# Two-dimensional long convolution with channel whitening: two buffers each for x and y, smaller y pieces, two-sided single groups and filler matmuls

## The chip, the cores and the metric

The kernel runs on one core of a Trainium2 chip. A core has a matrix engine (TensorE, PE in the profile), three engines for elementwise work (VectorE or DVE, ScalarE or ACT, GpSimd or POOL), a queue engine SP that issues transfers, and 16 DMA engines that move bytes between the device memory and the on-chip memory of 128 partitions. The metric is the time of one execution on the device, in microseconds. Lower is better.

## The reference

Everything is float32. The input `x` has 4 images, 64 channels and 256 x 256 pixels. Two small networks make a filter for each channel: `hx` and `hy`, 256 taps each. The kernel of a channel is their outer product, so the two-dimensional causal convolution separates into one along the rows and one along the columns. A second layer decorrelates the channels.

```
def filter(z, w1, b1, w2, b2, w3, b3, wo, freq):
    h = sin(freq * (z @ w1 + b1))
    h = sin(freq * (h @ w2 + b2))
    h = sin(freq * (h @ w3 + b3))
    return (h @ wo) * decay

k = outer(hx, hy) per channel                      # 256 x 256
y = irfft2(rfft2(x, 512) * rfft2(k, 512) / 512)[:256, :256] + x * bias

x1 = y with channels first, (64, 4*256*256)
x1_s = x1[:, ::9]                                  # every ninth pixel
mean1 = mean(x1_s)
cov = x1_s @ x1_s.T / n + 0.01 * I                  # x1_s as it is, mean not taken off
deconv = inverse square root of cov, five Newton-Schulz steps
out = deconv @ (x1 - mean1), back as (4, 64, 256, 256)
```

## The kernel before

**Filters.** At the start, six matmuls (line 147) with sines between them make the taps of all channels; two more (line 162) finish them. The taps go to device memory, as the array `g_d` and, for the first two channels, `g0_d` (lines 164 to 166).

**Convolution.** A convolution with 256 taps is a product with a triangular Toeplitz matrix. `load_toeplitz` (line 173) reads overlapping rows of the taps so that each partition holds a shifted copy. Channels come in 8 blocks of 8 (`g`), a block's matrices being one tile of a pool of three buffers. A step is one block of one image, `(g, n)`; there are 32. In the step order, blocks 0 to 5 run over the four images each; then each image has blocks 6 and 7. A step has four positions, `c` = 0, 2, 4, 6, of two channels each. In this text, (28, 4) is position c = 4 of step number 28.

At each position `group` (line 320) runs two jobs at once on TensorE. The first is the product along one axis for the present item (`p1`), the second is the product along the other axis for the item two positions earlier (`p2`). `toeplitz_products` (line 188) puts one job on the upper 64 rows of the array and the other on the lower 64 and swaps them with each tap block `k`. The order of `k` alternates from group to group. Between tap blocks a GpSimd no-op (line 224) keeps two halves from writing to the same bank at once. ScalarE copies `p1` to the tile `o1` with its halves swapped (line 338); VectorE adds `x * bias` to `p2` and writes `y` (line 343). VectorE also takes the samples for the covariance with nine masked copies for each step (line 252), some after each group. The first two groups have no second job and the last two no first job. In those, one half of the array has nothing to do at any time.

**Queues.** Within the convolution every engine keeps the order of the program text. After the instructions of a group, SP issues the store of `y` for the second item (line 353), then one load of `x` (line 103), then, in some groups, a Toeplitz load (line 178) and an early load of a finished piece of `y` (line 290). A DMA instruction waits on SP until its source is ready and its target free, and all that stands behind it waits too. `x` and `y` have three buffers each. The `x` load issued at c = 2 of step i is the first quarter of step i + 2:

```
part = (c - 2) // 2 % 4
to = i + 2 if c else i + 1
```

**Whitening.** After the last step come the last covariance (line 266) and a chain of small products, which give the matrix `W`. `y` is then read back in 32 pieces of 128 partitions by 4096 columns (2 MB), two images in one array `y_d[v]`, 64 channels each. `homes` (line 280) lists 13 buffers, by then unused by the convolution, for the first 13 pieces. Eight are loaded while the convolution still runs, at the positions in `early` (line 311), five after it. For each piece TensorE multiplies by `W` (line 521), ScalarE and VectorE add the shift (lines 526 and 529), and GpSimd issues the store to the output (line 534). A buffer is loaded again when its store is done.

Of the kernel before, what the change touches and what calls it, by code (L numbers as in the profile page):

```python
# [37 lines left out]
F32 = mybir.dt.float32  # L38
I32 = mybir.dt.int32
AF = mybir.ActivationFunctionType  # L40
ALU = mybir.AluOpType
AX = mybir.AxisListType
AFTER = mybir.DependencyInfo(mybir.DependencyClass.Sync, mybir.DependencyReason.DATA)

NB, C, L = 4, 64, 256
P, H2 = 128, 2
EMB, ORDER = 33, 64
PIX = L * L
CG = 8
HP = P // 2  # L50
# [5 lines left out]
GW = P + L  # L56
FP = 4096
# [8 lines left out]
def conv_whiten_kernel(ctx: ExitStack, tc: tile.TileContext, a: dict, out: bass.AP):  # L66
    nc = tc.nc
    x = a["x"]

    const = ctx.enter_context(tc.tile_pool(name="const", bufs=1))  # L70
    big = ctx.enter_context(tc.tile_pool(name="big", bufs=3))
    spool = ctx.enter_context(tc.tile_pool(name="spool", bufs=NB))
    tpool = ctx.enter_context(tc.tile_pool(name="tpool", bufs=3))
    o1pool = ctx.enter_context(tc.tile_pool(name="o1pool", bufs=4))
    dram = ctx.enter_context(tc.tile_pool(name="dram", bufs=1, space=bass.MemoryType.DRAM))
    psA = ctx.enter_context(tc.tile_pool(name="psA", bufs=8, space=bass.MemoryType.PSUM))

    y_d = [dram.tile([2 * C, PIX], F32, tag=f"y{v}", name=f"y_d{v}") for v in range(NB // 2)]
    g_d = dram.tile([P, GW], F32, tag="g", name="g_d")
    g0_d = dram.tile([2, 2, GW], F32, tag="g0", name="g0_d")  # L80

# [56 lines left out]
    nc.scalar.activation(bf[:, 1:2], bf[:, 0:1], AF.Sin)  # L140
    freq = cols[:, 3:4]
    nc.vector.tensor_scalar(bf, cols[:, 0:3], freq, None, ALU.mult)
    hs, wt = [zw[:, u * P : (u + 1) * P] for u in range(2)], zw[:, L : L + P]
    for i in range(3):
        for u in range(2):
            pm = psA.tile([P, P], F32, tag="psA", name=f"pm{i}_{u}")
            nc.tensor.matmul(pm, lhsT=wt, rhs=hs[u], start=True, stop=True)  # L147
            half = slice(u * P, (u + 1) * P)
            arg, k, nxt = (scratch[:, 2 + 3 * i + v, half] for v in range(3))
            nc.scalar.activation(arg, pm, AF.Identity, bias=bf[:, i : i + 1], scale=freq)  # L150
            nc.vector.tensor_scalar(k, arg, 1.0 / (2.0 * math.pi), MAGIC, ALU.mult, ALU.add)
            nc.vector.tensor_scalar(k, k, MAGIC, None, ALU.subtract)
            for part in (TP1, TP2):
                nc.vector.scalar_tensor_tensor(arg, k, -part, arg, ALU.mult, ALU.add)  # L154
            nc.vector.tensor_scalar(arg, arg, 3.1415925, -3.1415925, ALU.min, ALU.max)
            nc.scalar.activation(nxt, arg, AF.Sin)  # L156
            hs[u] = nxt
        wt = wbd[:, i * P : (i + 1) * P]
    for u in range(2):
        half = slice(u * P, (u + 1) * P)  # L160
        pf = psA.tile([P, P], F32, tag="psA", name=f"pf{u}")
        nc.tensor.matmul(pf, lhsT=wt, rhs=hs[u], start=True, stop=True)
        nc.vector.tensor_tensor(taps[:, half], pf, decay[:, half], ALU.mult)
    for f, queue in enumerate((nc.sync, nc.scalar)):
        queue.dma_start(out=g0_d[f], in_=taps[f * C : f * C + 2])
    nc.scalar.dma_start(out=g_d, in_=taps)

    def new_toeplitz(g):

# [1 line left out]
        return tpool.tile([P, 2, CG, L], F32, tag="toep", name=f"toep_{g}")  # L171

    def load_toeplitz(t, g, f, half, lo=0, hi=CG):
        source, row = (g0_d, 2 * f) if g == 0 and hi == 2 else (g_d, f * C + g * CG + lo)


        skip = 0 if f == half else HP
        nc.sync.dma_start(
            out=t[half * HP : (half + 1) * HP, f, lo:hi, skip:],
            in_=bass.AP(  # L180
                tensor=source.tensor,
                offset=source.offset + row * GW + skip,
                ap=[[1, HP], [GW, hi - lo], [1, L - skip]],
            ),
        )


    def toeplitz_products(units, ks):
# [3 lines left out]
        for k in ks:  # L192

            w = HP if k == L // HP - 1 else P
            for u, unit in enumerate(units):
                ends = []
                for m in range(H2):
                    for q in range(0, P, w):
                        for low in range(2):


                            job = unit[(k + low) % 2]
                            if job is None:
                                continue
                            ps, src, t = job
                            parts = slice(low * HP, (low + 1) * HP)
                            stop = HP * k - 1 if k else None
                            mm = nc.tensor.matmul(  # L208
# [13 lines left out]
                if k != ks[-1]:  # L222

                    fence[u] = nc.gpsimd.nop()  # L224
                    for name in ends:
                        tc.add_manual_dep(fence[u].ins, name, AFTER, reason="row tiles")

    def pack_by_pe(g, n, yt, cs):

# [30 lines left out]
    def covariance(n):  # L260
# [13 lines left out]
        nc.vector.scalar_tensor_tensor(cov, pc, 1.0 / NSAMP, cov, ALU.mult, ALU.add)  # L274


    pieces = [(v, q) for v in range(NB // 2) for q in range(PIX // FP)]


    homes = [  # L280
        {"t": (tpool, "toep"), "s": (spool, "samp"), "i": (big, "in"), "o": (big, "out")}[k]
        for k in "tssioitsoitos"
    ]

    def load_y(i):

        v, q = pieces[i]
        pool, tag = homes[i % len(homes)]
        t = pool.tile([P, FP], F32, tag=tag, name=f"yi_{v}_{q}")
        nc.sync.dma_start(out=t, in_=y_d[v][:, q * FP : (q + 1) * FP])  # L290
        return t

    def load_next():
# [6 lines left out]
    def bank(name):  # L300
        return psA.tile([P, H2, L], F32, tag="psA", name=name)
# [6 lines left out]
            k = first + (part * 12 // 8 if g < C // CG - 2 else part)  # L308
            blocks[k // 4, k % 4 * 2] = (g, part)

    early = {(28, 4): 1, (28, 6): 1, (29, 6): 1, (30, 4): 1, (31, 2): 1, (31, 4): 1, (31, 6): 2}
    orders = [list(range(L // HP)), list(reversed(range(L // HP)))]

    def pack(time=math.inf):
        while todo and time > 0:
            cost, op = todo.pop(0)
            op()
            time -= cost

    def group(first, second):  # L320

        units = [[None, None] for _ in range(2)]
        for u in range(2):
            if second is not None:
                g, n, c, _, _, o1s = second
                units[u][1] = (bank(f"p2_{g}_{n}_{c + u}"), o1s[u], toep[g][:, 1, c + u, :])
            if first is not None:
                g, n, c, xt, _, _ = first
                units[u][0] = (bank(f"p1_{g}_{n}_{c + u}"), xt[:, c + u], toep[g][:, 0, c + u, :])

        toeplitz_products(units, orders[0])
        orders.reverse()
        for u in range(2):
            if first is not None:
                g, n, c, _, _, o1s = first
                o1 = o1pool.tile([P, H2, L], F32, tag="o1", name=f"o1_{g}_{n}_{c + u}")
                for to, fr in ((slice(0, HP), slice(HP, P)), (slice(HP, P), slice(0, HP))):
                    nc.scalar.copy(o1[to], units[u][0][0][fr])  # L338
                o1s.append(o1)
            if second is not None:  # L340
                g, n, c, xt, yt, _ = second
                ch = g * CG + c + u
                nc.vector.scalar_tensor_tensor(  # L343
                    yt[:, c + u], xt[:, c + u], bias[:, ch : ch + 1], units[u][1][0],
                    ALU.mult, ALU.add,
                )

        pack(2.5)
        if second is not None:
            g, n, c, _, yt, _ = second  # L350
            last = (g, n) == steps[-1]
            row = n % 2 * C + g * CG + c
            nc.sync.dma_start(
                out=y_d[n // 2][row : row + 2, :].rearrange(
                    "c (b p w) -> p (c b) w", p=P, w=L
                ),
                in_=yt[:, c : c + 2].rearrange("p c b w -> p (c b) w"),
            )
            if last and c == CG // 2 - 2 or not last and c == CG - 2:
                todo.extend(pack_ops(g, n, yt, slice(0, c + 2)))  # L360

    engines = mybir.EngineType
    with tc.manual_schedule(
        engines={engines.PE, engines.SP, engines.DVE, engines.Activation, engines.Pool}
    ):
        toep = {0: new_toeplitz(0)}
        for lo, hi in ((0, 2), (2, CG)):
            for part in range(4):
                load_toeplitz(toep[0], 0, part // 2, part % 2, lo, hi)
        for c in range(0, CG, 2):  # L370
            load_x(loaded_x[steps[1]], *steps[1], c)
        for i, (g, n) in enumerate(steps):
            xt = loaded_x.pop((g, n))
            yt = big.tile([P, CG, H2, L], F32, tag="out", name=f"y_{g}_{n}")
            for c in range(0, CG, 2):
                item = (g, n, c, xt, yt, [])
                if g == C // CG - 1 and n > 0 and c == 4:
                    covariance(n - 1)
                group(item, pending.pop(0) if len(pending) == 2 else None)
                pending.append(item)  # L380
                if i == 0 and c == 6:

# [3 lines left out]
                    for u in range(2):  # L386
                        nc.vector.tensor_copy(twice[:, u], ident[0:C, 0:C])

                part = (c - 2) // 2 % 4
                to = i + 2 if c else i + 1  # L390
                if to < len(steps) and to > 1:
                    if part == 0:
                        loaded_x[steps[to]] = new_x(*steps[to])
                    load_x(loaded_x[steps[to]], *steps[to], 2 * part)
# [7 lines left out]
                    load_next()  # L402
        g, n, c, xt, yt, _ = pending[0]
        for item in pending:
            group(None, item)

        pack()
        pack_by_pe(g, n, yt, slice(CG // 2, CG))
# [95 lines left out]


    halves = [slice(u * C, (u + 1) * C) for u in range(2)]
    for i, (v, q) in enumerate(pieces):
        yt = loaded.pop(i)
        o = out[2 * v : 2 * v + 2].rearrange("u c h w -> (u c) (h w)")[:, q * FP : (q + 1) * FP]

        part = FP if 1 < i < len(pieces) - 2 else FP // 4
        for w in range(FP // 1024):


            po = [
                psA.tile([P, 512], F32, tag="psA", name=f"po_{v}_{q}_{w}_{u}") for u in range(2)
            ]
            cols = [slice((2 * w + k) * 512, (2 * w + k + 1) * 512) for k in range(2)]
            for k in range(2):
# [73 lines left out]
```

## Time and profile before

| | |
|---|---|
| median of 3 runs | 928.11 us (927.27 to 928.23) |
| the profiled execution | 930.36 us, span 928.2 us |
| PE busy | 788.6 us, 85% |
| DVE busy | 653.6 us, 70% |
| ACT busy | 480.9 us, 52% |
| DMA | 285.56 MB, mean 308 GB/s |
| first convolution matmul | 20.72 us |
| last convolution group's bias-add | 636.63 us |
| first whitening product | about 664 us |

The span is the part of an execution that the profile covers. Digits in a slice row are tenths of 1/40 of the span (23.2 us). An engine name with a q, such as SPq, stands for its queue of DMA instructions. A busy PE is not always PE at its best, since the time of one matmul in the trace includes its latency; matmuls that follow each other closely overlap. The clock row holds what the records of granted clock say; the first such record lies at about 40 us, and what came before is to be read from the spacing of the matmuls.

### The profile page before, as it was taken

The numbers are of one execution on the slowest core, as the hardware profiler recorded it, in microseconds if no ns is written. First come the engines' busy times: TensorE is split into PE (matmuls) and PEld (weight loads), VectorE is DVE, ScalarE is ACT, GpSimd is POOL, SyncE is SP. The second block draws the span as 40 slices with busy tenths as digits, with TensorE's granted clock in tenths as the row PEclk, the third lists the DMA queues.
The fourth block names the chain that finished last, engine by engine and source line by source line (L and its number), as shares of the span: only waits on it lengthen the run. The fifth ranks groups of instructions, "written<-read, shape, count | busy, mean of one in ns | idle before, by whom it ended". The sixth has DMA issues, their size and how long they took to land.

```text
span 928.2 us, 27807 instructions
## 1 busy us (share of the span) xinstructions
PE 788.6 (85%) x11814; PEld 631.0 (68%) x11814; DVE 653.6 (70%) x869; ACT 480.9 (52%) x791; POOL 31.8 (3%) x71
## 2 busy tenths in 40 slices
PE   3999999999999999999999999999787777765400
PEld 2899999999999999999999999998311111111100
DVE  3058687768777877787677866667599999996500
ACT  2345454545454544554554544441399888876500
POOL 3000000000000000000000000000010000000010
PEclk9999999999999999999999999999799999998755
DMA  4698888888888888879997769989999999999998
GB/s 145 189 275 257 251 258 261 248 258 258 252 251 262 260 248 261 262 237 280 284 277 236 234 189 332 326 288 392 417 407 429 430 428 429 431 430 431 431 430 340
DMA packets 115406, 285.56 MB, mean 308 GB/s; under 512 B 6831, under 2 KB 89172, under 8 KB 107604
## 3 DMA queue, kind: packets, MB, share of 16 engines
q1 hardware_dynamic: 108080, 216.08, 70.2%
q0 software_dynamic: 6336, 67.11, 17.0%
q8 instruction: 93, 1.52, 0.7%
q10 hardware_dynamic: 868, 0.60, 0.2%
q14 instruction: 29, 0.24, 0.1%
HBM read 149.35 MB, written 134.42 MB: 306 GB/s over the span
## 4 chain that ended last, share of the span: by engine, by line
PE 69%; issue 15%; DVE 9%; ACT 3%; DMA 2%; POOL 0%; POOLq 0%; ACTq 0%; DVEq 0%; SPq 0%
PE p L208 65%; DVE yi L529 8%; ACT yi L526 3%; DMA yi<-y_d 2%; PE pc L266 2%; PE pk L234 1%; POOL out_dram L534 0%; PE po L521 0%; DMA toep<-g_d 0%; DVE y L343 0%; PE ZY L436 0%; PE YT L436 0%; DVE scratch L154 0%; DVE samp L252 0%; PE pm L147 0%
## 5 line engine op out<-in xcount | busy, mean ns | idle before, releaser
L208 PE MATMUL p<-toep,x 64*64 64x64 f32 (+3 forms) x5120 | 595.6, 288 | 5.2 <-DMA toep<-g_d 4.7
L208 PE MATMUL p<-toep,o 64*64 64x64 f32 (+3 forms) x5120 | 589.2, 285 | 0.2
L208 PEld LDWEIGHTS p<-toep,x 64*128 64x128 f32 (+1 forms) x5120 | 548.3, 168 | 31.5 <-issue 5.6
L208 PEld LDWEIGHTS p<-toep,o 64*128 64x128 f32 (+1 forms) x5120 | 543.5, 166 | 11.8 <-POOLq L224 0.6
L338 ACT COPY o<-p 64x512 f32<-64x512 f32 x512 | 297.0, 580 | 317.9 <-PE p L208 310.1
L343 DVE SCALAR_TENSOR_TENSOR y<-x,bias,p 128x512 f32<-128x512 f32 x256 | 179.9, 743 | 162.7 <-PE p L208 162.2
L252 DVE COPY_PREDICATED samp<-mask,y 128x448 f32<-128x448 int32 (+3 forms) x288 | 281.0, 976 | 6.6
L529 DVE TENSOR_SCALAR yi<-po,shift 64x512 f32<-64x512 f32 x256 | 192.1, 750 | 23.4 <-PE po L521 16.7
L521 PE MATMUL po<-yi,W 64*64 64x512 f32 x1024 | 150.0, 653 | 63.1 <-DVE yi L529 40.9
L526 ACT ACTIVATE yi<-po,shift 64x512 f32<-64x512 f32 x256 | 174.9, 683 | 42.4 <-PE po L521 34.9
L521 PEld LDWEIGHTS po<-yi,W 64*64 64x64 f32 x1024 | 35.4, 141 | 176.9 <-DVE yi L529 127.8
L534 POOL DMA_DIRECT2D out_dram<-yi x44 | 23.7, 539 | 262.6 <-DVE yi L529 119.3
L420 POOL MEMSET chain<- 64x64 f32 x1 | 0.1, 146 | 616.6 <-PE p L208 616.6
L266 PEld LDWEIGHTS pc<-samp 128*64 128x64 f32 x464 | 14.4, 137 | 2.2 <-issue 1.4
L266 PE MATMUL pc<-samp 128*64 128x65 f32 x464 | 15.1, 223 | 0.7 <-ACT samp L243 0.4
L147 PE MATMUL pm<-scratch 128*128 128x128 f32 (+1 forms) x12 | 3.7, 466 | 8.8 <-ACT scratch L156 6.2
L274 DVE SCALAR_TENSOR_TENSOR cov<-pc,cov 128x65 f32<-128x65 f32 x4 | 0.9, 226 | 12.7 <-PE pc L266 12.7
L147 PEld LDWEIGHTS pm<-scratch 128*128 128x128 f32 (+1 forms) x12 | 2.9, 313 | 9.4 <-ACT scratch L156 6.8
L234 PE MATMUL pk<-y,pick 128*128 128x112 f32 (+1 forms) x36 | 7.7, 390 | 1.3 <-DVE y L343 1.3
L234 PEld LDWEIGHTS pk<-y,pick 128*128 128x128 f32 x36 | 7.3, 259 | 1.7 <-issue 1.7
L243 ACT COPY samp<-pk 128x116 f32<-128x116 f32 x1 | 0.3, 271 | 15.9 <-PE pk L234 15.9
L131 POOL TENSOR_SCALAR pick<-ident,rows 128x128 f32<-128x128 f32 x9 | 5.7, 649 | 0.0
(71 smaller groups left out, 41.8 us busy)
## 6 DMA issues: line engine op xcount, KB each, us to landing
x<-in_x_dram SPq DMA_DIRECT2D x128, 512.0 KB, 5.8
y_d<-y SPq DMA_DIRECT2D x128, 512.0 KB, 4.1
yi<-y_d SPq DMA_DIRECT2D x32, 2048.0 KB, 16.0
out_dram<-yi POOLq DMA_DIRECT2D x28, 2048.0 KB, 43.4
out_dram<-yi POOLq DMA_DIRECT2D x16, 512.0 KB, 8.4
toep<-g_d SPq DMA_DIRECT2D x28, 256.0 KB, 6.3
toep<-g_d SPq DMA_DIRECT2D x28, 192.0 KB, 5.7
toep<-g_d SPq DMA_DIRECT2D x2, 384.0 KB, 8.3
```

Source lines behind the costliest of these rows:

```text
L131: nc.gpsimd.tensor_scalar(pick[:, s, :], ident, rows[:, s : s + 1], None, ALU.mult)
L147: nc.tensor.matmul(pm, lhsT=wt, rhs=hs[u], start=True, stop=True)
L208: mm = nc.tensor.matmul(ps[q : q + w, m, HP * k : L], lhsT=src[parts, k // 2, m * P + q : m * P + q + w], rhs=t[parts, : stop : -1] if k e ...
L234: nc.tensor.matmul(pk[:, b, :, 0:nj], lhsT=pick[:, (s - b) % STEP, :], rhs=yt[:, cs, b, s : s + STEP * (nj - 1) + 1 : STEP], start=(s == 0 ...
L252: nc.vector.copy_predicated(dst, m, src)
L266: nc.tensor.matmul(pc[half], lhsT=samp[n][:, b, j, 0:C], rhs=samp[n][:, b, j, :], start=(b == 0 and j < 2), stop=(b == H2 - 1 and j >= NJ ...
L338: nc.scalar.copy(o1[to], units[u][0][0][fr])
L343: nc.vector.scalar_tensor_tensor(yt[:, c + u], xt[:, c + u], bias[:, ch : ch + 1], units[u][1][0], ALU.mult, ALU.add,)
L521: nc.tensor.matmul(po[u][halves[k]], lhsT=W[halves[u]], rhs=yt[halves[u], cols[k]], start=True, stop=True,)
L526: nc.scalar.activation(yt[halves[0], cols[k]], po[0][halves[k]], AF.Identity, bias=shift[halves[k]])
L529: nc.vector.tensor_scalar(yt[halves[1], cols[k]], po[1][halves[k]], shift[halves[k]], None, ALU.add)
L534: nc.gpsimd.dma_start(out=o[:, end - part : end], in_=yt[:, end - part : end])
```

## The change

- `x` and `y` (the tags "in" and "out") have two buffers each for three. The memory that this frees is a new pool of two tiles, which the convolution never uses; they are the first two of the 13 homes.
- `y_d` is one array for each image, with the upper and lower half of the image as the two sets of 64 partitions. A piece belongs to one image. Early loads start at (26, 4), two steps sooner; there are still eight. The store of `y` in a group becomes two DMAs, one for each half. The output has the same layout as these arrays and is put in order on the host.
- The `x` load after a group is now for the next step at c = 4 and 6, and for the present step at c = 0 and 2.
- The two first and two last groups use `half_group`, which puts both channels of the only job on both halves of the array at once, in four banks, with a fence for each bank.
- Block 0's Toeplitz matrices come in 14 loads of two or four channels in the order in which the groups use them, for 8. `g0_d` is stored by one DMA.
- Between the filter layers TensorE multiplies a tile of zeros: 8, 10 and 9 times, and 20 times after the last.

```
-    big = ctx.enter_context(tc.tile_pool(name="big", bufs=3))
+    big = ctx.enter_context(tc.tile_pool(name="big", bufs=2))
+    epool = ctx.enter_context(tc.tile_pool(name="epool", bufs=2))
-    y_d = [dram.tile([2 * C, PIX], F32, tag=f"y{v}", name=f"y_d{v}") for v in range(NB // 2)]
+    y_d = [dram.tile([H2 * C, PIX // H2], F32, tag=f"y{n}", name=f"y_d{n}") for n in range(NB)]
...
+    idle = o1pool.tile([P, H2 * L], F32, tag="o1", name="idle")
+    nc.vector.memset(idle, 0.0)
+    def busy(times):
+        p = psA.tile([P, P], F32, tag="psA", name="busy")
+        for _ in range(times):
+            nc.tensor.matmul(p, lhsT=idle[:, 0:P], rhs=idle[:, P : 2 * P], start=True, stop=True)
...
         wt = wbd[:, i * P : (i + 1) * P]
+        busy((8, 10, 9)[i])
...
-    for f, queue in enumerate((nc.sync, nc.scalar)):
-        queue.dma_start(out=g0_d[f], in_=taps[f * C : f * C + 2])
+    nc.sync.dma_start(out=g0_d, in_=taps[0:2])
     nc.scalar.dma_start(out=g_d, in_=taps)
+    busy(20)
...
+    def toeplitz_alone(jobs, which):
+        fence = {}
+        for step in range(L // HP):
+            for m in range(H2):
+                for u, (ps, src, t) in enumerate(jobs):
+                    k = step ^ u
+                    low = (k + which) % 2
+                    parts = slice(low * HP, (low + 1) * HP)
+                    stop = HP * k - 1 if k else None
+                    mm = nc.tensor.matmul(
+                        ps[m][:, HP * k : L],
+                        lhsT=src[parts, k // 2, m * P : (m + 1) * P],
+                        rhs=t[parts, : stop : -1] if k else t[parts, ::-1],
+                        start=(step == 0),
+                        stop=(step == L // HP - 1),
+                        skip_group_check=True,
+                    )
+                    if step:
+                        tc.add_manual_dep(mm.ins, fence[m, u].ins.name, AFTER, reason="row tiles")
+                    if step < L // HP - 1:
+                        fence[m, u] = nc.gpsimd.nop()
+                        tc.add_manual_dep(fence[m, u].ins, mm.ins.name, AFTER, reason="row tiles")
...
-        for k in "tssioitsoitos"
+        for k in "eetssitsoiots"
...
-    early = {(28, 4): 1, (28, 6): 1, (29, 6): 1, (30, 4): 1, (31, 2): 1, (31, 4): 1, (31, 6): 2}
+    early = {(26, 4): 1, (26, 6): 1, (27, 4): 1, (28, 2): 1, (29, 6): 1, (31, 4): 2, (31, 6): 1}
...
+        for b in range(H2):
+            row = b * C + g * CG + c
             nc.sync.dma_start(
+                out=y_d[n][row : row + 2, :].rearrange("c (p w) -> p c w", w=L),
+                in_=yt[:, c : c + 2, b],
             )
...
-        for lo, hi in ((0, 2), (2, CG)):
-            for part in range(4):
-                load_toeplitz(toep[0], 0, part // 2, part % 2, lo, hi)
+        for f, lo, hi in ((0, 0, 2), (0, 2, 4), (0, 4, 6), (1, 0, 2), (0, 6, 8), (1, 2, 4), (1, 4, 8)):
+            for half in range(2):
+                load_toeplitz(toep[0], 0, f, half, lo, hi)
...
-                group(item, pending.pop(0) if len(pending) == 2 else None)
+                if len(pending) == 2:
+                    group(item, pending.pop(0))
+                else:
+                    half_group(item, 0)
...
-                part = (c - 2) // 2 % 4
-                to = i + 2 if c else i + 1
-                if to < len(steps) and to > 1:
+                part = (c - 4) // 2 % 4
+                to = i + 1 if c >= 4 else i
+                if 1 < to < len(steps):
...
         for item in pending:
-            group(None, item)
+            half_group(item, 1)
+            pack(1.0)
+            store(item)
```

## The prediction

> **What bounds the kernel now.** I read the busy table by slices first, then the chain, then busy times by stage.
>
> ```profile
> PE   3999999999999999999999999999787777765400
> DMA  4698888888888888879997769989999999999998
> GB/s 145 189 275 257 251 258 261 248 258 258 252 251 262 260 248 261 262 237 280 284 277 236 234 189 332 326 288 392 417 407 429 430 428 429 431 430 431 431 430 340
> ...
> PE 69%; issue 15%; DVE 9%; ACT 3%; DMA 2%; POOL 0%; POOLq 0%; ACTq 0%; DVEq 0%; SPq 0%
> ```
>
> There are two regimes. To about 631 us TensorE is full and is 65 of the chain's 69% (line 208). From about 640 us the DMA engines are full at 430 GB/s, while TensorE drops to 5 to 7 tenths. By stage (columns: stretch, length, then busy us of PE, its weight loads, DVE, ACT, POOL, then clock, DMA share, GB/s):
>
> ```profile
> 300.00:400.00 100.00, 100.00 (x1710) 94.09 (x1714) 78.19 (x95) 50.45 (x87) 0.00 (x0) 1.00 0.85 255
> 712.00:790.00 78.00, 55.44 (x407) 11.30 (x406) 75.62 (x102) 68.84 (x101) 6.41 (x12) 1.00 1.01 430
> ```
>
> So a convolution group (two channels' first products with two other channels' second) costs what TensorE takes, and the whitening pass costs bytes: it ends when 430 GB/s have moved what is left. Groups: 126 double ones from 35.2 us to about 622, less three covariances of 3.64 us: (587 - 11)/126 = 4.57 us.
>
> What decides this change is one group's timetable:
>
> ```profile
> 248.31 1.61 DVE L343 SCALAR_TENSOR_TENSOR y<-x,bias,p 128x512 f32<-128x512 f32 x2 [0.15 <-PE p L208]
> ...
> 249.95 0.38 SPq L353 DMA_DIRECT2D y_d<-y  x1
> 250.38 0.50 SPq L103 DMA_DIRECT2D x<-in_x_dram  x1
> ...
> 253.77 0.24 PE L208 MATMUL p<-toep,o 64*64 64x64 f32 x1
> ```
>
> The lines come from three answers of the timeline, DVE's, SP's and PE's. TensorE finishes a group near 248.9 (midway through the 64x256 products that end it and begin the next), VectorE adds the bias until 249.92, SP stores y at 249.95 and issues an x load at 250.38. TensorE has meanwhile run the next group and starts the one after it near 253.7. Landing of x loads, from issue, in 240 to 260 us (no Toeplitz load near) and in 260 to 280 us (with them):
>
> ```profile
> DMA to landing us min/median/max: 4.6/4.7/4.8
> ...
> DMA to landing us min/median/max: 5.9/5.9/5.9
> ```
>
> The load of 250.38 lands near 255.1. Before, it is meant for a group seven places later, so this costs nothing.
>
> **The change, part by part.**
>
> *x with two buffers.* A load of part p of the next step was issued after the group at c=2 of the step two earlier; now it is issued after the group at c=4 of the step before (parts 2 and 3 in the step itself). Each load is thus issued behind group j's stores and used by group j+2. Only group j+1 lies between. Line 353's store stands ahead of it on SP and waits for VectorE's bias-add of group j (SP waits 387 us there in all), so it cannot go out earlier. Let D be the time from the end of group j to the landing: 250.38 - 248.9 = 1.5, plus 4.7, is 6.2 us; by the Toeplitz row 1.5 + 5.9 = 7.4. Available: 4.57. TensorE is late in every group, and D + 4.57 is what two groups then take: (6.2 + 4.57)/2 = 5.39 us, or 5.99. The store is now two DMAs, one per half: 0.43 us more on SP ahead of the x load. As x's bytes queue behind y's anyway, this adds between 0 and 0.43 to D. At the dear end p = 6.2. Loads for steps 2 to 31: 30 x 4 = 120 groups. Cheap end (5.39 - 4.57) x 120 = 98 us, dear end 1.63 x 120 = 196. I take D = 6.53, p = 5.55 and **+118**: nearer the cheap row, since longer groups leave the DMA queue time to empty, and the Toeplitz row suffers from leftovers of the group before.
>
> A rule speaks otherwise here. The Trainium skill, "DMA: Bandwidth & Descriptors", section "Anatomy of one DMA — SWDGE (gpsimd) path", fits a lone transfer as 2.0 us plus bytes over 436 GB/s: 3.2 us for 512 KB (an estimate, and for the other queue kind). Then D = 4.7, p = 4.64 and the cost is only +8. I take the row: it has the store's 512 KB ahead of x in the same queue, as the changed kernel will.
>
> *Early y loads in the queue.* Eight 2 MB loads stay eight, but five ((26,4), (26,6), (27,4), (28,2), (29,6)) now precede x loads that have no slack. 2 MB at 430 GB/s are 4.9 us; begun when x's own bytes are done, some 4 us after its issue, they end about 2.6 us after the next store could begin. The group waiting for that x feels 2.6, its neighbour 1.6 (it had 1.0 to spare): about 2.1 each, **+10** (0 to 25). The load at (26,4) also waits on SP for image 0's last stores, and the next group's stores and x load stand behind it; those stores land in 3.3 to 4.2 us and a group lasts longer, so no wait.
>
> *Two y buffers.* A y buffer is written again eight groups later; its stores land in 4.1 us and its nine sample copies are spread over the three groups after its last store. No wait: 0. It frees the memory for the two extra buffers.
>
> *Start.* Two single-sided groups ran alone at half clock:
>
> ```profile
> 20.72 15.09 PE L208 MATMUL p<-toep,x 64*128 64x256 f32 x79 [4.71 <-DMA toep<-g_d]
> 35.61 0.63 PE L208 MATMUL p<-toep,x 64*128 64x256 f32 x1
> ...
> 248.43 0.38 PE L208 MATMUL p<-toep,x 64*128 64x256 f32 x1
> ```
>
> 64x256 pieces of one row half start 0.43 us apart at 36 us and 0.21 later. The first two groups take 14.5 us. On both halves a group is four rounds, paired 256 with 192 and 128 with 64 columns: 2 x 2 x (0.21 + 0.21 + 0.11 + 0.11) = 2.6 us warm, 5.1 cold, plus three fences through POOL of at most 0.6 (the 0.57 and 0.61 us stalls at 24.6 and 26.3). Warm I take 3.5 each: -7.5; cold 6: -2.5. The third group, 35.2 to 42, becomes warm: -2.2. Here the Trainium skill, "TensorE: Matmul & The Clock Gate", Part 1, says that about 3.4 us of sustained matmuls release the clock; by that the old start would have been warm at 24.1 and warming worth 1.7 us. The trace measures half rate until 38.5, so I use the row. The fillers' cost: 20 matmuls of 128x128 at 0.21 (0.43 cold) are 4.3 (8.6) us in the 4.7 us gap before the first Toeplitz landing, so 0 to +4; 8, 10 and 9 in gaps of 3.85, 2.37 and 2.12 us, 0 to +4 together. Shorter layer matmuls and the earlier first block give about 0.5 back. Block 0's loads become 14 for 8, SP issues of about 0.65: the eighth, which the third group needs, is out near 23, in time. Sum of the start: **-10** (-14 to 0).
>
> *End of the convolution.* Two last groups of 4.3 become about 3.4, **-2**. Covariances fall partly into TensorE's new idle time: **-3**.
>
> *Whitening pass.* Pieces of one image keep 2 MB and 16 KB rows, and the output is as many bytes: 0. Before, the 13 buffers were still filling until about 673 us although the matrix was ready at 664: some 3.8 MB, 9 us at 430 GB/s. With idle DMA in a stretched convolution all 13 are full when the matrix is; writes alone then run at VectorE's pace (262 KB per 0.75 us, 350 GB/s) for some 10 us, which takes 2 back, and starting takes 2: **-5** (-9 to 0). Cover: if the convolution were not stretched, starting the loads two steps earlier gives about as much.
>
> Sum: 118 + 10 - 10 - 2 - 3 - 5 = **+108**. The profiled execution took 930.4 around a span of 928.2, so its span agrees with the runs' median of 928.1 and the execution lies 2.3 above it. Added to the median: **1036 us**.
>
> **Rivals.**
> 1. *Late x, as above*: 1036, own range 1005 to 1095. For it: 255.1 against 253.7 in the timetable, in the row that is cheapest.
> 2. *x in time, faster.* If x landed within 4.57 us of a group's end, nothing would be late: -10 - 2 - 5 and about -3 for earlier y loads give 908. For it: the DMA engines are nearly idle from 255.2 to 255.9 us (share 0.06), so bandwidth is to be had. Against it: the 4.7 was measured with them idle (0.16) just before the store. It decides only at a landing under 3.1 us from issue; the smallest seen is 4.4.
> 3. *A small lateness*: DMA latency falls to the lone-transfer estimate: 940 to 1005.
> 4. *More than late*: stalls also cool TensorE. The clock-gate page, "Why this matters for your kernels", warns of gaps over about 3 us; mine average 1.0 and would be 2 if every second group bore them. The 712 to 790 row has TensorE 71% busy at clock 1.00, so I expect none; with clock losses, or the dear ends together, 1095 to 1150.
> 5. *The warming does nothing and the loads are hidden anyway*: within 0.2%.
>
> **How the numbers follow.** Case 1 0.76, case 2 0.10, case 3 0.06, case 4 0.06, case 5 0.02. Slower 0.76 + 0.06 + 0.06 = 0.88; faster 0.10; same 0.02, where 0.2% is about what a measurement of this kernel can tell. The range 980 to 1095 takes case 1 and the upper part of case 3.
>
> **What would show it.** Right: from about 55 us TensorE's line waits on DMA x, some 1 us per group and 110 to 130 us in all; groups in pairs of 11 us; DMA share in the convolution down from 0.85 to about 0.72; the third group at about 27 us with 64x256 pieces 0.21 apart; whitening from matrix to end about 259 us for 264. Wrong: x lines that come ahead of the stores on SP, x landings of 3 us, or a clock under 1.00 in the convolution. The size is wrong if the store's two DMAs delay x by a full issue, or if the early loads hold it for their whole 5 us.

## The result and the profile after

The changed kernel takes **1170.1 us** (median of 4 runs, 1163.8 to 1171.5) where the kernel before takes 928.2. The ratio is 1.259, 95% interval 1.254 to 1.264. The direction was forecast; the size was not: +242 us for a predicted +108, and beyond the range, which ended at 1095.

The page of the changed kernel has these slices (TensorE, its granted clock, DMA share, rate; a slice is now 29.2 us) and this chain by engine; the first line is the clock row of the kernel before:

```profile
PEclk9999999999999999999999999999799999998755
...
PE   8888877887778878778887787878897877776520
...
PEclk9989988888999888999888889989897999998855
DMA  5755656455566555674555656775669999999998
GB/s 159 231 166 173 194 178 186 157 166 169 168 205 185 168 154 164 201 206 145 177 179 174 176 165 202 269 266 177 223 222 412 392 430 429 429 430 429 431 431 349
...
PE 41%; DMA 23%; DVE 18%; issue 14%; SPq 3%; ACT 0%; POOL 0%; POOLq 0%; DVEq 0%; ACTq 0%
```

TensorE was full in the convolution and is now at 7 or 8 tenths, the DMA engines have gone down with it, and a clock that had stood at 9 throughout the convolution falls to 8 again and again. DMA, 2% of the chain before, is 23%. In the stage rows (same columns as in the prediction) the stretch that had 100 of 100 us busy at full clock has 77 at 0.88, with a DMA share of 0.55:

```profile
200.00:300.00 100.00, 77.04 (x1122) 72.01 (x1120) 49.78 (x61) 34.12 (x59) 0.00 (x0) 0.88 0.55 168
903.00:1169.00 266.00, 151.91 (x1024) 36.20 (x1021) 192.10 (x257) 174.96 (x256) 23.63 (x44) 0.85 0.99 418
```

The waits of the changed kernel name the transfer:

```profile
PE p L216 <- DMA x<-in_x_dram: 144.4, 60, 4.5
PEld p L216 <- issue: 78.8, 29, 4.6
PEld p L216 <- DVE samp L314: 78.0, 26, 4.1
```

TensorE's sixty waits are one for each pair of groups, and they last 2.4 us each. The two lines of the weight load cover the same gaps; VectorE's samples merely ended last before them.

Where the 241 us of span went: the double groups run from 26.40 us to a last bias-add that ends at 877.4, 851.0 us, for 602.9 before (35.19 to 638.05), so **+248**; they begin 8.8 us sooner; what follows takes 292.2 for 290.1, +2.

One pair of groups in the changed kernel's timeline, from SP's and TensorE's answers:

```profile
381.61 1.23 SPq L413 DMA_DIRECT2D y_d<-y  x2
382.89 0.49 SPq L104 DMA_DIRECT2D x<-in_x_dram  x1
...
387.51 0.76 PE L216 MATMUL p<-toep,x 64*128 64x256 f32 x1 [2.56 <-DMA x<-in_x_dram]
388.07 0.63 PE L216 MATMUL p<-toep,x 64*128 64x256 f32 x1
...
391.03 0.32 PE L216 MATMUL p<-toep,x 64*128 64x192 f32 x1
...
395.26 1.53 SPq L413 DMA_DIRECT2D y_d<-y  x2
```

Group j ended near 380.2. The x load behind it, for group j+2, went out at 382.9 and landed at 387.5: TensorE stood still for 2.56 us. Then comes what I had put in a rival: from the second on, the 64x256 pieces after the gap start 0.43 us apart (0.63 us each), half rate, until 391. This group's products start at 387.5 and the next group's at 393.8, 6.3 us, where a group takes 4.57. The profile's records of the granted clock hold only full and half; one at half lies from 387.5 to 390.9. There are 39 such half-clock entries before 880 us, 157 us in all (154 of them before the last bias-add); in the kernel before, none lies between 40 and 630 us.

### The profile page after: what moved, and what is told of

It reads as the page before. It is cut to its first block, busy times and chain, and to the rows that moved or that the text cites. A ratio compares the mean times of both kernels' runs of the same rounds, so it can differ in the third digit from the quotient of the medians.

```text
span 1169.6 us, 28135 instructions
## 1 busy us (share of the span) xinstructions
PE 883.2 (76%) x11876; PEld 716.7 (61%) x11876; DVE 658.7 (56%) x882; ACT 479.0 (41%) x791; POOL 31.6 (3%) x71
## 4 chain that ended last, share of the span: by engine, by line
PE 41%; DMA 23%; DVE 18%; issue 14%; SPq 3%; ACT 0%; POOL 0%; POOLq 0%; DVEq 0%; ACTq 0%
PE p L216 37%; DMA x<-in_x_dram 22%; DVE yi L593 9%; DVE y L400 5%; SPq L413 3%; DVE samp L314 2%; PE pc L328 1%; PE ph L248 1%; PE pk L296 1%; POOL out_dram L598 0%; PE po L585 0%; DMA toep<-g_d 0%; DVE y L285 0%; DMA y_d<-y 0%; DVE scratch L164 0%
## 5 line engine op out<-in xcount | busy, mean ns | idle before, releaser
L216 PE MATMUL p<-toep,x 64*64 64x64 f32 (+3 forms) x5040 | 669.7, 302 | 158.4 <-DMA x<-in_x_dram 144.4
L216 PEld LDWEIGHTS p<-toep,x 64*128 64x128 f32 (+1 forms) x5040 | 582.5, 177 | 194.4 <-issue 78.8
L216 PE MATMUL p<-toep,o 64*64 64x64 f32 (+3 forms) x5040 | 665.6, 303 | 0.0
L216 PEld LDWEIGHTS p<-toep,o 64*128 64x128 f32 (+1 forms) x5040 | 587.3, 178 | 8.5
L397 ACT COPY o<-p 64x512 f32<-64x512 f32 x504 | 292.3, 580 | 550.0 <-PE p L216 542.2
L151 PE MATMUL busy<-idle 128*128 128x128 f32 x94 | 13.0, 302 | 0.0
L151 PEld LDWEIGHTS busy<-idle 128*128 128x128 f32 x94 | 12.5, 216 | 0.2 <-issue 0.2
L282 DVE COPY o<-ph 64x256 f32<-64x256 f32 x8 | 3.4, 421 | 9.2 <-PE ph L248 9.0
L282 ACT COPY o<-ph 64x256 f32<-64x256 f32 x8 | 2.9, 366 | 10.1 <-PE ph L248 10.0
```

What stands on the lines that cost most here:

```text
L151: nc.tensor.matmul(p, lhsT=idle[:, 0:P], rhs=idle[:, P : 2 * P], start=True, stop=True)
L216: mm = nc.tensor.matmul(ps[q : q + w, m, HP * k : L], lhsT=src[parts, k // 2, m * P + q : m * P + q + w], rhs=t[parts, : stop : -1] if k e ...
```

## The experiments

The theory: every loss comes from the x load that is issued one group before its use, once as waiting and once more through the clock. The rivals: some other part of the change (split stores, two y buffers, the arrays per image) causes it; or the clock changes but costs nothing, the transfers setting the period alone.

**The load one group sooner, all else of the change kept.**

```
-                part = (c - 4) // 2 % 4
-                to = i + 1 if c >= 4 else i
+                part = (c - 2) // 2 % 4
+                to = i + 1 if c else i
```

> The changed kernel with each x load issued one group sooner (first quarter of the next step after c = 2, so that two groups lie between issue and use instead of one). Theory, late x and all that follows from it: the waits on x (144 us) and the half-clock windows in the convolution (157 us) go away; the third group still starts 8.8 us sooner than before and warm (2 more), so 910 to 918 us. Rival, the loss comes from something else in the change (two DMAs per store, one array per image, two y buffers, the fences): above 1100 us.

Measured 927.3 us, ratio 0.9992 (0.9979 to 1.0005): not the rival's 1100, and not the 910 to 918 expected. All 242 us are gone, so the split stores, the arrays and the fences cost nothing that lasts. But the gain of the start, which stood at 11 to 12 us in this trace until 530 us, is gone at the end too. (This kernel is called the one with a lead of two groups below.) In its waits between 528 and 612 us, while early y loads run, stand

```profile
PE p L216 <- DMA x<-in_x_dram: 6.6, 3, 2.5
...
DVE y L400 <- DMA y_d<-y: 3.6, 1, 3.6
```

and the row of 500 to 605 us has TensorE busy 98.4 us at clock 0.95. The second line looks like the two y buffers, but it is not: this bias-add starts at 554.35, when TensorE's next group starts (554.35), so it waited for its own group's products, and a store happened to land at 554.5.

**The early loads behind the last x load**, in the same kernel.

```
-    early = {(26, 4): 1, (26, 6): 1, (27, 4): 1, (28, 2): 1, (29, 6): 1, (31, 4): 2, (31, 6): 1}
+    early = {(31, 4): 7, (31, 6): 1}
```

> The kernel with the x load one group sooner, and all eight early y loads moved behind the last x load (seven at (31, 4), one at (31, 6)). The total is not the test: five loads of 2.1 MB then fall into the full stretch, some 20 us. If the early loads are what cost that kernel its start-up gain: no TensorE wait on x and no half-clock window between 500 and 605 us, and the first whitening bias-add some 10 us sooner than its 664.4 us, near 654. If a lead of two groups is too short in itself: still 660 or later.

In the one execution, 500 to 605 us has TensorE busy 105.0 of 105 us at clock 1.00 and no wait on x or y; the first whitening bias-add starts at 654.4 us, as expected. The total is 942.9, since the moved bytes fall into the full stretch. So it was the early loads that took the start's gain from the kernel with a lead of two groups.

**The late load alone, in the kernel before** (three buffers, one store).

```
-                part = (c - 2) // 2 % 4
-                to = i + 2 if c else i + 1
+                part = (c - 4) // 2 % 4
+                to = i + 1 if c >= 4 else i
```

> The kernel before with nothing changed but the place of the x load: the same late issue as in the changed kernel, three buffers kept, one DMA per store. Theory, late x alone: about the changed kernel's 1170 us plus the 11 us that its start gained, less up to 26 us if the second store DMA had put x back by 0.43 us in each pair of groups: 1150 to 1185, with PE waits on x of some 130 to 150 us. Rival, the other parts cause the loss: 928.

Measured 1144.3 us, ratio 1.232 (1.227 to 1.238), TensorE's waits on x 133 us, half-clock entries 109 us before the last bias-add. This moved load makes 216 of the 242 us by itself. It lies 6 us under the expected stretch.

**The same with the store in two DMAs.**

```
+            for b in range(H2):
                 nc.sync.dma_start(
-                    out=y_d[n // 2][row : row + 2, :] ...
+                    out=y_d[n // 2][row : row + 2, b * P * L : (b + 1) * P * L] ...
```

> As the kernel before with the late x load, and the store of y split into its two halves as in the changed kernel. If the second DMA puts the x load back by its full issue time: 26 us more than the kernel with the late load alone (0.43 us in each of 60 pairs), or more with the clock. If x's bytes stand behind y's anyway: the same within 5 us.

Measured 1167.6 us, ratio 1.258 (1.252 to 1.263), 23.3 more. That is near the 26 of a full issue, but the traces divide it otherwise. A pair consists of the group that starts after a stop of TensorE and of D, from this group's end to the start after the next stop. Over the pairs before the first early load (52 and 50), D grows only from 7.32 to 7.43 us: the x load goes out 0.7 us later after the first store (1.14 for 0.43), but lands sooner after its issue (on average 4.8 us for 5.2 over the loads whose landing the traces have). The group after the stop grows from 5.59 to 5.92 us, and half-clock time from 109 to 154 us. By these averages 7 us of sixty pairs are lateness and 20 the clock's. That the sum is near a full issue is chance.

**Fillers ahead of each double group.** They write into the group's own bank, where the group's first product replaces them, and wait for no x. First six, then three.

```
+        for _ in range(FILL):
+            nc.tensor.matmul(
+                units[0][0][0][:, 0, 0:P], lhsT=ident, rhs=ident, start=True, stop=True
+            )
         toeplitz_products(units, orders[0])
```

> The changed kernel with six 128x128 products of the identity ahead of each double group, into the group's own bank (overwritten by the group's first product), which do not wait for x and so keep TensorE busy in part of each gap. Theory, the gaps cost a second time through the clock: half-clock windows go from 157 us to near 0 and the time falls by half of them, to 1085 to 1105, although TensorE has 160 us more work. Rival, the period of a pair is set by the transfers alone and the clock does not matter: 1170, or more by the fillers' own time.

Six: 1142.5 us, not the 1085 to 1105 expected. The clock held (4 us of half-clock entries before the last bias-add), but TensorE now has no gap left: each filler block takes about 1.6 us, two in a pair, more than the gap. This run could not price the clock.

> The changed kernel with three fillers ahead of each double group instead of six (six held the clock but took 1.55 us in both groups of a pair, 3.1 us, more than the gap of about 2.4). Theory, a pair is the lateness D of about 7.1 us plus one group of 4.7 at full clock once the clock holds: 11.8 us for 13.5, sixty pairs, so 1050 to 1085, half-clock windows in the convolution under 40 us. Rival, the clock is worth only the 28 us that six fillers gave: 1125 to 1145.

Three: 1123.8 us, ratio 1.210 (1.208 to 1.213). Half-clock entries before the last bias-add fall from 154 to 17 us, and between 60 and 700 us the clock is 1.00 for 0.90. Its clock row:

```profile
PEclk9999999999999999999999999989996999998755
```

The time falls by 46 us. That is below the rival's stretch of 1125 by 1 us and far above mine. One pair in this kernel's timeline (TensorE and SP):

```profile
205.63 0.94 PE L394 MATMUL p<-ident 128*128 128x128 f32 x6
206.96 0.87 SPq L418 DMA_DIRECT2D y_d<-y  x2
207.93 0.44 SPq L105 DMA_DIRECT2D x<-in_x_dram  x1
212.50 0.48 PE L217 MATMUL p<-toep,x 64*128 64x256 f32 x1 [0.33 <-DMA x<-in_x_dram]
...
217.31 0.94 PE L394 MATMUL p<-ident 128*128 128x128 f32 x6
```

A group ends when the next fillers start. From 205.63 to the store 1.33 us; two stores to the x load 0.97; to TensorE's start 4.57; the group 4.81. At full clock, D is 6.9 here and 7.5 and 7.4 in the next two pairs. From SP's x loads of 50 pairs before the first early load, a pair takes on average 9.18 us in the kernel before, 12.27 with three fillers, 13.44 in the changed kernel, 12.96 and 13.34 in the two kernels before with the late load. So the fillers save 58.5 us in these 50 pairs. They give back 5.9 at the start, where their kernel issues its ninth x load that much later, and 6.5 behind these pairs, with the early loads; 46 are left.

**The change with x left as it was**: three x buffers, seven groups ahead; two y buffers and one extra home.

```
+    xpool = ctx.enter_context(tc.tile_pool(name="xpool", bufs=3))
-    epool = ctx.enter_context(tc.tile_pool(name="epool", bufs=2))
+    epool = ctx.enter_context(tc.tile_pool(name="epool", bufs=1))
-        for k in "eetssitsoiots"
+        for k in "etssitisoiots"
-    early = {(26, 4): 1, (26, 6): 1, (27, 4): 1, (28, 2): 1, (29, 6): 1, (31, 4): 2, (31, 6): 1}
+    early = {(26, 4): 1, (26, 6): 1, (28, 2): 1, (29, 6): 1, (30, 4): 1, (31, 2): 1, (31, 4): 1, (31, 6): 1}
-                part = (c - 4) // 2 % 4
-                to = i + 1 if c >= 4 else i
+                part = (c - 2) // 2 % 4
+                to = i + 2 if c else i + 1
```

> The whole change except that x keeps three buffers and its old place (seven groups ahead); one extra home buffer instead of two, so the memory and the 13 homes stay; the same eight early loads, starting at (26, 4). Theory, in the kernel with the load one group sooner the early loads still pushed x past its use (10 us lost between 533 and 605 us); with seven groups they cannot: the convolution ends 10 to 11 us sooner than before and, as the whitening pass costs bytes, the whole takes 912 to 920. Rival, the whitening pass takes back what the convolution gains: 925 to 928.

Measured **916.7 us**, ratio 0.9875 (0.9855 to 0.9895): faster than both kernels. Its stage rows have TensorE full at full clock, and its whitening pass is about 263 us:

```profile
60.00:500.00 440.00, 440.00 (x7692) 413.92 (x7692) 338.34 (x409) 223.15 (x385) 0.00 (x0) 1.00 0.85 259
...
652.00:914.00 262.00, 147.09 (x1020) 34.70 (x1012) 192.09 (x256) 174.92 (x256) 23.64 (x44) 0.86 0.98 415
```

**The start, in two halves.** The fillers between the filter layers alone, in the kernel before; and the last kernel without them.

```
+        busy((8, 10, 9)[i])
...
+    busy(20)
```

> The kernel before with the filler matmuls between the filter layers alone. By the row (half rate until 38.5 us): the single-sided groups run warm, 14.5 us become about 8 and the third group saves 2: 918 to 921. By the rule of 3.4 us of warming: 926.5. If single-sided groups let the clock fall again: 926 to 928.

924.3 us, ratio 0.9954 (0.9937 to 0.9972), between the expected stretches. Its TensorE lines explain it:

```profile
19.89 4.41 PE L219 MATMUL p<-toep,x 64*128 64x256 f32 x40 [0.37 <-DMA toep<-g_d]
26.04 1.21 PE L219 MATMUL p<-toep,x 64*64 64x64 f32 x19 [1.74 <-DMA toep<-g_d]
...
31.65 0.63 PE L219 MATMUL p<-toep,x 64*128 64x256 f32 x1
```

The first single-sided group is warm (4.4 us), the second waits for a Toeplitz block that the old order brings late, and the clock falls to half from 28.2 to 35.1 us.

> As the kernel with three x buffers, without the fillers between the filter layers: the two-sided single groups then start cold. By the row: 5.1 us plus fences each for 3.1, and part of the third group, so 4 to 7 us slower than with the fillers. By the rule of 3.4 us: 1.7 us slower.

919.8 us, 3.1 more than with the fillers, less than the row's 4 to 7 and more than the rule's 1.7. The four times of each kernel do not overlap, but only just (917.9 to 921.1, and 915.2 to 917.8). Without the fillers the third group starts at 28.93 us for 26.27; the two-sided groups began at 21.00 cold and the clock record turns to full at 25.6.

## Why the prediction was wrong

**The mechanism was right.** Each x load stood behind the stores, and TensorE waited for it once in each pair of groups. The kernel before with only that edit is 23% slower; with the load one group sooner, or with x left as it was, the loss is gone.

**Two terms of the sum failed, by about the same amount.** I had 11.1 us for a pair of groups. In the changed kernel, 46 pairs before the first early load take 13.46 us on average, a D of 7.48 (6.5 to 9.2) and a group of 5.98 after the stop. (D is taken to TensorE's start, 0.1 us behind the landing.) The 2.36 us too little are 142 us in sixty pairs; the result lies 134 beyond the forecast.

1. *D, the lateness at full clock.* I took 6.53 us; 7.48 is 0.95 more, 57 us in sixty pairs. The step that failed is the choice "nearer the cheap row". That row, 240 to 260 us, was not typical: its median landing of 4.7 us is the lowest, and those of thirteen other stretches between 120 and 500 us are 5.0 to 6.6. In the kernel before, the time from a group's end to the landing of the x load behind it is 7.35 us on average over the 46 loads of this stage whose landing the trace has, under 6.5 in 10 of them: 1.24 to the store, 0.44 to the x load, 5.67 to the landing. The pages have the medians of all x loads, before and after:

```profile
x<-in_x_dram SPq DMA_DIRECT2D x128, 512.0 KB, 5.8
...
x<-in_x_dram SPq DMA_DIRECT2D x128, 512.0 KB, 5.0
```

So x did land sooner after its issue when the queue had time to empty, as I argued, but the second store's issue took most of that back. My dear end, +196 us, is also what the kernel with three fillers shows, 1124 - 928 = 196, though that sum holds the other terms too. At full clock the group after a stop takes 4.73 us for my 4.57, another 10 us.

2. *The clock.* I put it at nothing. The group after a stop takes 5.98 us on average and 4.73 where no half-clock entry falls in it (16 of the 46): 1.25 us a pair, 75 us if all sixty pairs bear it. Removing it with fillers gained 58.5 us in 50 pairs, and 46 in the whole, where the fillers' own cost is taken off. Rival 4 was right in kind, and I gave it 6 in 100. I argued from mean gaps of 1.0 us, "2 if every second group bore them", against a rule of about 3 us. Every second group does bear them, and 2.3 us (the median of 62 gaps) is enough. The row of 712 to 790 us, which I took as a sign against it, has 22.6 us of idle time in 78, on average 1.0 us in 3.41.

**The trace tells when the clock falls.** I cut eight runs' convolutions (the kernel before, the changed one, and the six of the experiments other than the two on the start and the one with moved early loads) from 60 us to the last bias-add, into stretches of 3.41 us at the times of the clock records (all of which fit such a grid) and counted in each the time with neither a matmul nor a weight load:

| idle in one stretch at full clock | stretches | next one at half clock |
|---|---|---|
| under 1.7 us | 1396 | 0 |
| 1.7 to 2.0 us | 30 | 9 |
| over 2.0 us | 103 | 102 |

It returns to full only after a stretch with almost no idle time: of 112 half-clock stretches with up to 0.5 us of it one was followed by another at half clock, of 17 with more all were. The Trainium skill, "TensorE: Matmul & The Clock Gate", Part 1, has the free-running window of 3413 ns, which these records fit, but asks for an idle window; its section "Why this matters for your kernels" asks for "No PE-idle gaps >~3µs between matmul bursts". Here 2 us of idle time in one window are enough, so that rule is not safe. A gap's length alone does not decide: in the changed kernel and the two kernels before with the late load, all 26 gaps of 2.0 to 2.6 us that lay inside one window were followed by half clock, and 17 of the 35 that a window's border cut in two. That the gaps cause the drops is shown by the fillers; that the windows' idle time is the measure is a count.

**The smaller terms.**
- *Early loads, +10*: nothing in the changed kernel. Its last pairs take 13.97 us for 10.13 before in the same place, a difference of 3.8, no more than the 4.3 of the earlier pairs. They cost their 10 us in the kernel with a lead of two groups instead.
- *Two y buffers, 0*: right. Three waits of VectorE are put down to stores of y (two with a lead of two groups, one in the kernel with x left as it was), and each ends when TensorE's next group starts, so it was for the products.
- *Start, -10*: right. The third group starts at 26.40 us (I said about 27) with pieces 0.21 apart.
- *Row against rule at the start*: the rule of 3.4 us of activity was closer than I made it. Two-sided groups from cold reach full clock 4.6 us after they begin, at the end of the first window that they fill, and the fillers are worth 3.1 us there. What stayed cold for 18 us were the single-sided groups, though from 22.3 to 35.9 us, four windows, the trace has at most 0.1 us in a window without a matmul or weight load. So the table above does not hold for them. Warming them alone gave 4.4 us, since the clock fell again, after a window with only 1.2 us of idle time.
- *Whitening, -5*: wrong, it is 266.8 us from the first product to the end for 264.3. Not all 13 buffers were full when the matrix was ready: three of the eight early loads come only after step 31's c = 4, and with the five behind them they are 17 MB. The DMA engines were still at 413 GB/s with them between 870 and 906 us.
- *DMA: the fitted 2.0 us plus bytes* of the skill's page gave +8 us for the late load, which cost 216. It is stated for a lone transfer of the other queue kind and does not carry over to loads that stand behind a store here.

The cases' chances: the faster one, 10 in 100, rested on a landing under 3.1 us; the shortest in the changed kernel was 4.0.

## What to carry to other kernels

When a load loses its slack, count from the end of the work that its queue waits for, through every DMA ahead of it, to the landing under load, and compare with the work in between: here 7.5 us against 4.6. Take the average over the stage for the landing, not one tidy place. A wait that comes in one piece each few microseconds costs a second time through TensorE's clock; spread the idle time, or cover it, so that no 3.4 us window has over 1.7 us of it. If memory has to be freed, take it from the buffer with slack: y lost its third buffer at no cost that these traces show, while x with two buffers lost the start's gain even at the longer lead, once the early loads ran.

## What the runs showed of the hardware

- TensorE's clock fell after 102 of 103 windows of 3.41 us with over 2.0 us of idle time and after none of 1396 with under 1.7, while TensorE ran groups on both row halves.
- A pair of the changed kernel takes 13.44 us on average, near four such windows (13.65), so gaps and windows can stay in step: half-clock entries begin at 592.3, 605.9, 619.6 and 633.2 us.
- A store split into two DMAs sent the load behind it out 0.7 us later, yet TensorE's wait for it ended only 0.1 us later after the group's end. The kernel became 23.3 us slower, most of it through half-clock time, which rose from 109 to 154 us.
- Products on one row half ran at half rate for 18 us, with at most 0.1 us of idle time in four windows of 3.41 us; both halves brought the clock up in 4.6 us. Whether the half array or the two stops of about 0.6 us at the fences kept the clock down was not separated.
